# Clearing the weights above the diagonal on GpSimd in attention's last steps

## The chip, the cores and the metric

The kernel runs on one core of a Trainium2 chip. A core has TensorE for matrix products (PE in the profile, its weight loads PEld), VectorE (DVE), ScalarE (ACT), GpSimd (POOL) and SyncE (SP), which here issues most of the DMAs. TensorE writes its products to PSUM; the other tiles lie in SBUF. Each engine works through its own queue in order, and waits for the others through semaphores. The metric is the device time of one execution in microseconds; the time of a kernel is the median of its runs.

## The reference

Two layers act on x of shape (2, 1024, 512), each adding an "attention" branch and a feed-forward branch of the normalized x. Only the second layer's attention matters here. It has 16 heads of 32 numbers, and position i may look at positions j up to i:

```python
scores = jnp.einsum('bqhe,bkhe->bhqk', q, k) * scale
causal = jnp.tril(jnp.ones((l, l), dtype=bool))
scores = jnp.where(causal[None, None], scores, -jnp.inf)
attn = jax.nn.softmax(scores, axis=-1)
out = jnp.einsum('bhqk,bkhe->bqhe', attn, v)
out = out.reshape(b, l, d) @ W_out.T + b_out
```

The rest of the layer is a gated feed-forward network of width 2048, whose hidden values are thinned to two of four before the last product. The first layer has a small recurrence in place of attention, and a feed-forward network with a Walsh-Hadamard transform.

## The kernel before

The kernel has three stages, one after the other: the first layer, then attention of the second, then its feed-forward network. Attention lies between about 653 and 1211 us of the profile.

**Units and steps.** Attention works on eight units `u`, each one batch element and four heads (tiles have 128 partitions: 4 heads of 32). Scores are held transposed, keys on the partitions and queries along the row. A step `(u, j, kt)` takes one block of 128 keys, `kt`, against a half `j` of 512 queries: 4 steps for j = 0 and 8 for j = 1, so `per` = 12 a unit and 96 in all. In the last four steps of a half, `kt >= 4 * j`, the block of keys meets the diagonal: `s` is the first query that sees it, and the 128 columns from `s` on hold the triangle.

**What a step does.** `weights` (from L1218) computes the scores of four heads on TensorE into two PSUM tiles of two heads each (L1226), and subtracts the row's shift by a small product (L1232); ScalarE takes the exponential of each tile into SBUF (L1243), as `acc` in a half's first step, else as `pt`, of which there are five buffers. On the diagonal the part of the tile that lies above it is then set to 0, in one of two ways. GpSimd's `affine_select` (L1252) keeps an element where column minus row is not negative, and writes 0 elsewhere. VectorE (L1248) takes the minimum with `allowed`, a constant triangle of 1e30 and 0. One step later `gather` multiplies the weights with the values on TensorE (`o`, L1276) and adds them to the running sums `acc` (`add_weights`, L1263). At the end of a half `total` (L1296) sums over the partitions by a product with ones, ScalarE copies that to `inv` (L1301, one buffer), VectorE takes its reciprocal in four quarters (L1306), and after the fourth GpSimd multiplies the half's output `att` with it (L1308).

**Which engine.** `idle_vector(u, j, kt)` is true when the step lies within the last `ahead` = 13: by then the maxima, a pass over the scores that runs 13 steps ahead and keeps VectorE occupied, are over. Where it is true, VectorE adds the running sums, else GpSimd (with one exception). With `kt - 1` in the call, VectorE clears the triangle in steps 84 to 95, which is unit 7.

**The order.** The loop over `n` writes out every engine's order by hand: `weights` of step n, then what is put in the middle of it, `gather` of step n - 1, the maxima of step n + 13, one part of a projection (`one_part`: a part is four products, and every second part ends with VectorE's addition of the result to x, L1318), then `what_is_fixed`, which issues the reciprocals (`divide`). `in_program_order` makes every engine keep that order. For unit 7's first half `total` comes in step 89, the reciprocals in steps 89 (two), 90 and 91, and the multiplication L1308 behind the fourth, in step 91.

`allowed` is made at the start of attention by a GpSimd memset and an `affine_select` (L974, L975), between those of `mask` and the constants after it.

Of the kernel before, what the change touches and what calls it, by code (L numbers as in the profile page):

```python
# [9 lines left out]
F32 = mybir.dt.float32  # L10
BF16 = mybir.dt.bfloat16
AF = mybir.ActivationFunctionType
ALU = mybir.AluOpType
PSUM = bass.MemoryType.PSUM

P = 128
# [15 lines left out]
MASKED = -1e30  # L32
# [3 lines left out]
def two_layers(ctx: ExitStack, tc: tile.TileContext, t: dict, out: bass.AP):  # L36
    nc = tc.nc
# [32 lines left out]
    def ps_wide(name):  # L70
        nonlocal wides
        wides += 1
        return ps_pair(name, wides % 3)
# [282 lines left out]
    with tc.tile_pool(name="a", bufs=1) as a:  # L356
# [39 lines left out]
        for name in ("dskip", "Wo_by"):  # L396
            factors[name] = row(f"{name}_tmp")
            nc.sync.dma_start(
                out=factors[name],
                in_=t[name].partition_broadcast(P) if name == "dskip" else t[name],  # L400
# [387 lines left out]
        for n in range(NU - 1):  # L788
            u = 2 * n + 2
# [41 lines left out]
        for base in (0, NU):  # L831
            i, d = 2 * base // NU, base + (1 if base else 3)
# [119 lines left out]
    with tc.tile_pool(name="b", bufs=1, reuse_waits="tile") as b:  # L952
# [7 lines left out]
            out=wv, in_=t["WqkvT"][:, 2 * D :].rearrange("(k p) c -> p k c", p=P)  # L960
# [8 lines left out]
            out=mask, in_=mask, compare_op=ALU.is_ge, fill=MASKED,  # L969
            base=0, pattern=[[-1, P]], channel_multiplier=1,  # L970
        )

        allowed = b.tile([P, P], F32, name="allowed")
        nc.gpsimd.memset(allowed, -MASKED)  # L974
        nc.gpsimd.affine_select(  # L975
            out=allowed, in_=allowed, compare_op=ALU.is_ge, fill=0.0,
            base=0, pattern=[[1, P]], channel_multiplier=-1,
        )
        identb = b.tile([P, P], BF16, name="identb")
        nc.vector.tensor_copy(identb, ident)  # L980
        onesb = b.tile([P, P], BF16, name="onesb")
# [231 lines left out]
        def idle_vector(u, j, kt):  # L1213

            return per * u + 4 * j + kt + ahead >= len(second)

        def weights(u, j, kt):

            q, k, neg = qk[u, 0], qk[u, 1], negs[u, j]
            name = f"{u}_{j}_{kt}"  # L1220
            s = max(0, kt - 4 * j) * P
            cols = slice(j * 512 + s, (j + 1) * 512)
            pair = [ps_wide(f"s_{name}_{p}") for p in range(2)]
            for h in range(4):
                rows = slice(h * HD, (h + 1) * HD)
                nc.tensor.matmul(  # L1226
                    pair[h // 2][:, h % 2, s:], k[rows, kt * P : (kt + 1) * P], q[rows, cols],
                    start=True, stop=False,
                )
            for h in range(4):  # L1230
                rows = slice(h * HD, h * HD + 3)
                nc.tensor.matmul(  # L1232
                    pair[h // 2][:, h % 2, s:], onesb[rows, :], neg[rows, s:],
                    start=False, stop=True,
                )
            got = []
            for p in range(2):

                if kt == 0:
                    pt = b.tile([P, 2, 512], F32, tag=f"acc{p}", name=f"acc_{name}_{p}", bufs=2)  # L1240
                else:
                    pt = b.tile([P, 2, 512], F32, tag="pt", name=f"pt_{name}_{p}", bufs=5)
                nc.scalar.activation(  # L1243
                    pt[:, :, s:], pair[p][:, :, s:], AF.Exp, scale=1.0 / math.sqrt(HD)
                )
                d = pt[:, :, s : s + P]
                if kt >= 4 * j and idle_vector(u, j, kt - 1):
                    nc.vector.tensor_tensor(  # L1248
                        d, d, allowed.unsqueeze(1).to_broadcast([P, 2, P]), ALU.min
                    )  # L1250
                elif kt >= 4 * j:
                    nc.gpsimd.affine_select(  # L1252
                        out=d, in_=d, compare_op=ALU.is_ge, fill=0.0,
                        base=0, pattern=[[0, 2], [1, P]], channel_multiplier=-1,
                    )
                got.append(pt)
            return u, j, kt, s, got
# [208 lines left out]
        for n in range(-ahead, len(second)):  # L1466
            if n == 0:
                alone = None
            now = weights(*second[n]) if n >= 0 else None
            for f, *args in middle.pop(n, ()):  # L1470
                f(*args)
            if behind is not None:
                gather(*behind)
            behind = now
            for f, *args in after.pop(n, ()):
                f(*args)
            if n < 0:
                one_part(n)
            if n + ahead < len(first):
                do_first(n + ahead)  # L1480
            while add_later:
                add_weights(*add_later.pop())
            if (n >= 0 or n % 2) and n not in quiet:
                one_part(n)
            while late(n) and one_part(n):
                pass
            what_is_fixed(n)
# [17 lines left out]
    with tc.tile_pool(name="c", bufs=1, reuse_waits="tile") as c_:  # L1505
# [131 lines left out]
        for n in range(groups - 1):  # L1637

            end = n == groups - 2
            u = 2 * n + 2  # L1640
# [165 lines left out]
```

## Time and profile before

| | us |
|---|---|
| median of three runs (lowest, highest) | 1796.81 (1796.33, 1798.09) |
| the profiled execution | 1798.73 |
| its span, first to last instruction | 1797.0 |

Instructions of the span that have to do with the triangle and with the sums around it (us from the span's start):

| line, engine | what | count | mean or median ns | where |
|---|---|---|---|---|
| L1252 POOL | selection, 128x256 | 112 | 409 | 727 to 1151 |
| L1248 DVE | minimum, 128x256 | 16 | 422 | 1151 to 1185 |
| L1263 POOL | running sums | 124 | 1770 | 737 to 1150 |
| L1263 DVE | running sums | 36 | 949 | 784 to 1187 |
| L1306 DVE | reciprocal of a quarter, 128x128 | 8 from 1150 to 1190 | 926 | |
| L1308 POOL | multiplication by the inverse, 128x512 | 2 from 1150 to 1190 | 1272 | 1164, 1174 |

Busy time of the engines in stretches of 10 us, and the clock granted to TensorE as a share of full speed:

| us | PE | DVE | ACT | POOL | clock |
|---|---|---|---|---|---|
| 1150 to 1160 | 9.13 | 8.69 | 7.58 | 1.68 | 1.00 |
| 1160 to 1170 | 9.59 | 7.93 | 7.53 | 1.27 | 1.00 |
| 1170 to 1180 | 8.21 | 10.00 | 3.69 | 1.27 | 0.83 |
| 1180 to 1190 | 9.75 | 7.17 | 2.33 | 0.00 | 1.00 |

How to read it: times of a group are those of its instructions' records, from start to end; a record contains time that the instruction stands still after it has started. In the timeline and the chain of waits a row has a start, a duration, an engine, the operation's line and what it writes and reads; in brackets stands how long the engine was idle before it, and what ended that. In the windows `0.82 (x4)` is a busy time and a number of instructions.

### The profile page before, as it was taken

The numbers are of one execution on the slowest core, as the hardware profiler recorded it, in microseconds if no ns is written. First come the engines' busy times: TensorE is split into PE (matmuls) and PEld (weight loads), VectorE is DVE, ScalarE is ACT, GpSimd is POOL, SyncE is SP. The second block draws the span as 40 slices with busy tenths as digits, with TensorE's granted clock in tenths as the row PEclk, the third lists the DMA queues.
The fourth block names the chain that finished last, engine by engine and source line by source line (L and its number), as shares of the span: only waits on it lengthen the run. The fifth ranks groups of instructions, "written<-read, shape, count | busy, mean of one in ns | idle before, by whom it ended". The sixth has DMA issues, their size and how long they took to land.

```text
span 1797.0 us, 19003 instructions
## 1 busy us (share of the span) xinstructions
PE 1772.6 (99%) x7354; PEld 909.9 (51%) x7354; DVE 1153.1 (64%) x1516; ACT 480.3 (27%) x687; POOL 836.0 (47%) x727
## 2 busy tenths in 40 slices
PE   9999999999999999999999999999999999999999
PEld 5456566555555564333333333334555555555555
DVE  4875444555544458576666767752867778768676
ACT  3322222122221113433443443412212211212220
POOL 5145553355642244577867866613243344243510
PEclk9999999999999999999999999999999999999999
DMA  6120110111101010000000000011011102201101
GB/s 235 47 82 24 47 43 28 36 36 36 36 24 36 12 41 13 1 12 13 1 24 25 13 12 1 25 47 43 28 59 35 48 24 72 87 29 47 47 1 47
DMA packets 29609, 68.12 MB, mean 38 GB/s; under 512 B 3408, under 2 KB 11856, under 8 KB 27984
## 3 DMA queue, kind: packets, MB, share of 16 engines
q1 hardware_dynamic: 28800, 66.61, 11.1%
q8 instruction: 59, 0.97, 0.2%
q10 hardware_dynamic: 720, 0.30, 0.1%
q14 instruction: 30, 0.25, 0.0%
HBM read 62.70 MB, written 4.19 MB: 37 GB/s over the span
## 4 chain that ended last, share of the span: by engine, by line
PE 90%; POOL 4%; DVE 3%; issue 2%; ACT 1%; ACTq 0%; POOLq 0%; DVEq 0%
PE p_a L183 22%; PE p_c L183 21%; PE d L309 19%; PE m L1169 4%; PE s L1226 3%; PE pv L1047 3%; POOL acc L1263 3%; PE pq_a L1122 3%; PE po L1047 3%; PE o L1276 3%; PE dr L1627 2%; PE pq_c L1122 1%; DVE tops L1177 1%; POOL pt L1252 1%; PE pp L607 1%
## 5 line engine op out<-in xcount | busy, mean ns | idle before, releaser
L327 POOL TENSOR_TENSOR x<-x,de 128x512 f32<-128x512 f32 x87 | 126.6, 1470 | 297.8 <-DVE x L322 162.2
L1263 POOL TENSOR_TENSOR acc<-acc,pt 128x1024 f32<-128x1024 f32 (+3 forms) x124 | 216.4, 1770 | 0.0
L1177 DVE TENSOR_REDUCE tops<-m 128x2 f32<-128x1024 f32 (+2 forms) x192 | 180.9, 956 | 52.3 <-PE m L1169 47.7
L322 DVE TENSOR_TENSOR x<-x,d 128x512 f32<-128x512 f32 x145 | 99.1, 684 | 143.0 <-PE d L309 142.7
L1243 ACT ACTIVATE pt<-s 128x1024 f32<-128x1024 f32 (+3 forms) x160 | 115.3, 766 | 190.1 <-PE s L1232 171.1
L309 PE MATMUL d<-td,h 128*128 128x256 f32 x592 | 139.2, 379 | 0.0
L309 PEld LDWEIGHTS d<-td,h 128*128 128x128 f32 x592 | 112.5, 190 | 42.6 <-issue 28.7
L183 PE MATMUL p_a<-xt,s_a 128*128 128x512 f32 x256 | 116.6, 598 | 0.0
L183 PE MATMUL p_a<-xt,w 128*128 128x512 f32 x256 | 115.4, 593 | 0.7 <-ACT xt L136 0.7
L183 PE MATMUL p_c<-xt,gu 128*128 128x512 f32 x256 | 115.7, 592 | 0.0
L183 PE MATMUL p_a<-t_a,s_a 128*128 128x512 f32 x256 | 115.3, 594 | 0.0
L183 PE MATMUL p_c<-xt,s_c 128*128 128x512 f32 x256 | 115.1, 592 | 0.0
L1169 PE MATMUL m<-qk,qk 32*128 32x512 f32 (+3 forms) x768 | 102.0, 538 | 3.7 <-ACT acc L1243 3.0
L1176 DVE TENSOR_TENSOR m<-m,mask 128x256 f32<-128x256 f32 x128 | 54.8, 428 | 72.4 <-PE m L1169 63.9
L1226 PE MATMUL s<-qk,qk 32*128 32x512 f32 (+3 forms) x768 | 97.7, 532 | 3.5 <-DVE tops L1177 2.3
L176 POOL TENSOR_TENSOR s_c<-gu,s_c 128x512 f32<-128x512 f32 x16 | 20.4, 1275 | 132.4 <-PE p_c L183 132.4
L183 PEld LDWEIGHTS p_a<-xt,s_a 128*128 128x128 f32 x256 | 47.3, 190 | 57.6 <-issue 57.1
L1169 PEld LDWEIGHTS m<-qk,qk 32*128 32x128 f32 x768 | 39.6, 184 | 71.7 <-issue 25.3
L1276 PE MATMUL o<-pt,v 128*32 128x512 f32 (+3 forms) x640 | 71.1, 482 | 4.2 <-POOL pt L1252 2.1
L183 PEld LDWEIGHTS p_c<-xt,s_c 128*128 128x128 f32 x256 | 48.6, 190 | 51.4 <-issue 50.2
L183 PEld LDWEIGHTS p_c<-xt,gu 128*128 128x128 f32 x256 | 48.6, 190 | 51.0 <-issue 49.5
L183 PEld LDWEIGHTS p_a<-xt,w 128*128 128x128 f32 x256 | 48.4, 190 | 50.1 <-issue 47.6
(286 smaller groups left out, 3216.2 us busy)
## 6 DMA issues: line engine op xcount, KB each, us to landing
w<-in_W SPq DMA_DIRECT2D x32, 512.0 KB, 3.5
gu<-in_gu SPq DMA_DIRECT2D x32, 512.0 KB, 3.5
wd<-in_down SPq DMA_DIRECT2D x8, 1024.0 KB, 4.9
x<-in_x SPq DMA_DIRECT2D x16, 256.0 KB, 4.2
w2h<-in_W2q SPq DMA_DIRECT2D x4, 1024.0 KB, 11.5
xr<-in_x SPq DMA_DIRECT2D x16, 256.0 KB, 2.7
wqk<-in_WqkvT SPq DMA_DIRECT2D x16, 256.0 KB, 3.0
out_x<-x SPq DMA_DIRECT2D x15, 256.0 KB, 2.0
```

The source lines that it names most:

```text
L183: nc.tensor.matmul(pair[:, m, :], a[:, m, k, :], x[:, k, :], start=start and k == 0, stop=stop and k == 1, skip_group_check=True,)
L309: nc.tensor.matmul(out_[:, j, :], lhs[:, q, j * P : (j + 1) * P], rhs[:, q], start=m in (0, 1, 3, 4) and j == q == 0, stop=j == q == 1, sk ...
L322: nc.vector.tensor_add(r, r, out_)
L327: nc.gpsimd.tensor_add(r, r, u2[half])
L1047: nc.tensor.matmul(got[0], lhs(k), rhs(k), start=(k == 0), stop=(k == KC - 1))
L1122: nc.tensor.matmul(got[chain], lhs[:, k, :], rhs[k] if type(rhs) is list else rhs[:, k, :], start=start and k == 0, stop=stop and k == 1, ...
L1169: nc.tensor.matmul(pair[h // 2][:, h % 2, :e], q[rows, qt * P : (qt + 1) * P], k[rows, c * 512 : c * 512 + e], start=True, stop=True,)
L1177: nc.vector.tensor_reduce(out=tops[u][:, c, qt, 2 * p : 2 * p + 2], in_=pair[p][:, :, :e], axis=mybir.AxisListType.X, op=ALU.max,)
L1226: nc.tensor.matmul(pair[h // 2][:, h % 2, s:], k[rows, kt * P : (kt + 1) * P], q[rows, cols], start=True, stop=False,)
L1243: nc.scalar.activation(pt[:, :, s:], pair[p][:, :, s:], AF.Exp, scale=1.0 / math.sqrt(HD))
L1263: eng.tensor_add(acc[:, :, s:], acc[:, :, s:], pt[:, :, s:])
L1276: nc.tensor.matmul(po[rows, s:], v[:, rows], pts[h // 2][:, h % 2, s:], start=(kt == 0), stop=last, tile_position=(0, h * HD),)
```

## The change

The selections of GpSimd take the place of VectorE's minima in steps 84 to 95 too. The constant `allowed` and the two instructions that make it are gone. Nothing else is edited; running sums stay where they were.

```diff
-        allowed = b.tile([P, P], F32, name="allowed")
-        nc.gpsimd.memset(allowed, -MASKED)
-        nc.gpsimd.affine_select(
-            out=allowed, in_=allowed, compare_op=ALU.is_ge, fill=0.0,
-            base=0, pattern=[[1, P]], channel_multiplier=-1,
-        )
...
                 d = pt[:, :, s : s + P]
-                if kt >= 4 * j and idle_vector(u, j, kt - 1):
-                    nc.vector.tensor_tensor(
-                        d, d, allowed.unsqueeze(1).to_broadcast([P, 2, P]), ALU.min
-                    )
-                elif kt >= 4 * j:
+                if kt >= 4 * j:
                     nc.gpsimd.affine_select(
                         out=d, in_=d, compare_op=ALU.is_ge, fill=0.0,
                         base=0, pattern=[[0, 2], [1, P]], channel_multiplier=-1,
                     )
```

## The prediction

> **What bounds the kernel now.** I read the shares on the page first, then the chain of waits over the stretch that the change touches, then the timeline and short windows there.
>
> ```profile
> PE 1772.6 (99%) x7354; PEld 909.9 (51%) x7354; DVE 1153.1 (64%) x1516; ACT 480.3 (27%) x687; POOL 836.0 (47%) x727
> ```
>
> TensorE is busy almost throughout, so a change on VectorE and GpSimd counts only where it opens or closes a hole in TensorE's row. The edited branch runs where `per*u + 4*j + kt - 1 + 13 >= 96`, that is for steps 84 to 95, unit 7 alone. Eight of its twelve steps lie on the diagonal, with two tiles each:
>
> ```profile
> L1248 DVE TENSOR_TENSOR pt<-pt,allowed x14: 357/422/1497, 1153.6 to 1185.0; 128x256 f32<-128x256 f32 x14
> L1248 DVE TENSOR_TENSOR acc<-acc,allowed x2: 411/418/424, 1151.4 to 1151.9; 128x256 f32<-128x256 f32 x2
> L1252 POOL TENSOR_SCALAR_AFFINE_SELECT pt<-pt x98: 398/409/881, 731.7 to 1150.3; 128x256 f32<-128x256 f32 x98
> ```
>
> So 16 minima of 0.42 us go and 16 selections of 0.41 us come, on the same 128x256 elements; these lines also give the stretch, 1151 to 1186 us. The chain of waits there (start, us, what):
>
> ```profile
> 1164.02 1.28 POOL att L1308
> 1165.33 0.59 ACT inv L1301
> 1165.95 1.76 DVE inv L1306 x2
> 1167.71 1.14 DVE acc L1263 x2
> ...
> 1172.99 0.86 DVE inv L1306
> 1173.85 1.71 DVE pt L1248 x2
> 1175.60 1.92 PE o L1276 x4
> 1177.52 2.57 PE po L1047 x4
> ```
>
> The reader is to see that from 1164 to 1175.6 the end is set by VectorE (reciprocals, running sums, then the minima of step 92, two in 1.71 us), and from 1175.60 by TensorE again. GpSimd meanwhile holds little: after 1152.4 the timeline has only two multiplications by the inverse (L1308), at 1164.02 and 1173.99, until 1194. On those counts the move looks like a relief. Two things speak against it.
>
> **First: the two engines exclude each other.** The trace of before shows this where VectorE's last borrowed sum met GpSimd (start, us, engine, line):
>
> ```profile
> 1147.73 1.82 POOL L1263 TENSOR_TENSOR acc<-acc,pt 128x768 f32<-128x768 f32 x1
> 1147.82 2.28 DVE L1263 TENSOR_TENSOR acc<-acc,pt 128x512 f32<-128x512 f32 x1
> 1149.49 0.88 POOL L1252 TENSOR_SCALAR_AFFINE_SELECT pt<-pt 128x256 f32<-128x256 f32 x1
> 1150.02 0.89 DVE L1263 TENSOR_TENSOR acc<-acc,pt 128x512 f32<-128x512 f32 x1
> 1150.32 0.85 POOL L1252 TENSOR_SCALAR_AFFINE_SELECT pt<-pt 128x256 f32<-128x256 f32 x1
> ```
>
> A 128x512 sum alone takes 0.65 us (two in 1.29 us at 1158.64). Here it took 2.28: it stood still until GpSimd's sum ended at 1149.5, then ran its 0.6. The selection behind it took 0.88 instead of 0.41, and so on in turns. The Trainium skill (SBUF — State Buffer, § Who interferes with whom) states the rule: a VectorE operation with two SBUF inputs and a GpSimd operation that reads SBUF need the same port, which the first to start holds for its whole instruction; the other stands still. Read by the durations alone (0.41 us on an idle engine), the VectorE queue between 1154.9 and 1163.9 loses its four minima of steps 86 and 87. Without them: copy of the shifts 0.40, sums of step 85 2 x 0.91, of step 86 2 x 0.65, two reciprocals 1.76, sums of step 87 2 x 0.39, two reciprocals 1.76: 7.82 us, from the end of the transposes at 1154.93 to 1162.75, against 1163.88 in the trace: a gain of 1.13 us. By the rule, the four selections run between these very sums and hold them up by 0.13 + 3 x 0.40 = 1.3 us: 1164.05, a loss of 0.2. The trace's own rows above decide for the second: I take **0** here, between -1.13 and +0.2. (The first selection, from 1155.07, has mostly run when the copy ends at 1155.33, hence 0.13.) Steps 84 and 85 cost nothing: their sums have no reader until 1156, and TensorE reads the tile of step 84 at 1152.59, 1153.1 for its second half, when the selection is done at 1152.57. Selection 86's second half comes at about 1156.8 instead of 1155.98; TensorE slips by some 0.5 us there, which the wait for ACT's copy of the inverse at 1165.33 (0.36 us of TensorE idle, 1.27 of weight loads) takes up.
>
> **Second: the queue of GpSimd.** The multiplication of unit 7's first half is issued in step 91, after the reciprocal of its last quarter, and the selections of step 92 stand behind it in GpSimd's queue. In before:
>
> ```profile
> 1173.99 1.27 POOL L1308 TENSOR_TENSOR att<-att,inv 128x512 f32<-128x512 f32 x1 [8.70 <-ACT pt L1243]
> 1174.05 1.50 DVE L1248 TENSOR_TENSOR pt<-pt,allowed 128x256 f32<-128x256 f32 x1
> ```
>
> The first minimum slipped in ahead of it (1173.77 to 1174.13), the second waited for it and ended at 1175.55. After the change, with times of before and strict turns:
> - The last reciprocal ends at 1173.8. Next on VectorE is a sum of step 91 (1.17 us, its tile ready since 1170.03); it takes the lock at once: to 1174.95.
> - The multiplication has it next: 1.27, to 1176.2.
> - The other sum, waiting since 1174.95: to 1177.4.
> - Selection of step 92, first half: to 1177.8; second half, nothing between: to 1178.2.
>
> So TensorE's second half of o starts at 1178.2 in place of 1175.60: **+2.6 us**, the first half at 1177.8 in place of 1174.18. TensorE has nothing else: its order puts o of step 92 ahead of the projection. Behind it, in one queue, wait o, the four projection products, and the scores of step 94.
>
> **What hangs on it: the clock.** (windows of 1 us: us, busy of PE, PEld, DVE, ACT, POOL, then the granted clock)
>
> ```profile
> 1173.00:1174.00 1.00, 0.00 (x0) 0.00 (x0) 1.00 (x2) 0.81 (x1) 0.01 (x1) 1.00 0.00 0
> 1174.00:1175.00 1.00, 0.82 (x4) 0.14 (x4) 1.00 (x2) 0.00 (x0) 1.00 (x1) 1.00 0.00 0
> 1175.00:1176.00 1.00, 0.64 (x4) 0.19 (x4) 1.00 (x2) 0.00 (x0) 0.27 (x1) 0.69 0.00 0
> 1176.00:1177.00 1.00, 1.00 (x4) 0.00 (x0) 1.00 (x2) 0.20 (x1) 0.00 (x0) 0.50 0.00 0
> ```
>
> The granted clock is 0.50 from about 1175.4 to 1178.8, and o's last four matmuls take 1.92 us where all eight take 1.06 at 1170.45, the four projection products 2.64 where others take 1.98: some 2 us are lost to the clock in before already. Afterwards TensorE is idle from 1172.75 to 1177.8, 5.1 us, so it resumes at half clock too. The Trainium skill (TensorE: Matmul & The Clock Gate, Part 1) has a free-running window of 3.4 us, after which the rate is set by how busy it was; the 3.4 us of this trace agree. If the window in which it resumes counts as idle, a second half-rate window follows. Half of 3.4 us, 1.7, is the most that this adds; the least is 0 (or a little below, if the two losses differ by phase). I take 0.4, near the low end, because before carries such a loss already and both depend on the phase.
>
> **Given back.** At 1184.85 a projection waited 0.25 us for VectorE's addition at L1318; with TensorE late, it has waited out: -0.25. The remaining sums (steps 92 to 95) run in turns with selections: 0.4 us each, but the sums end at about 1189.1 and the product of ones with them (L1296) stands at 1189.03 + 2.7 in TensorE's order, so they stay hidden; were they 2.6 us later still, they would be paid one for one. The tail has no other hole: TensorE runs without a gap from 1190 to 1221, and GpSimd's weight sums, done at 1200.66, are needed at 1214.
>
> **The removed constant** is a 0.21 us memset and a 0.30 us selection on GpSimd at 653, before an idle time of 2.19 us on that engine: 0. Its 512 bytes per partition shift the tiles allocated after it; no row bears on what this does, and I count nothing.
>
> **Sum:** 0 + 2.6 + 0.4 - 0.25 = +2.7 us (bounds: -0.6 with no lock; +4.4 with the whole clock window and 0.2 in the first part). The profiled execution took 1798.73 us (span 1797.0 and 1.73 around it), so 1801.4 by itself; it is the slow end of the runs shown, whose median is 1796.81. Against the median: **1799.5 us**.
>
> **The rivals.**
> - *Second cold window* (24%): as above with the full 1.7 us of clock: +4.0 to +4.4, 1801.1. For it: the window from 1175.4 to 1178.8 would hold 1 us of TensorE work of 3.4, and the one before it, with 1.6, was followed by half rate. Against: its phase is free.
> - *The multiplication goes first* (16%): GpSimd keeps the lock from its multiplication (1173.99 to 1175.26) through both selections, to 1176.05: +0.45 us at o, 1797.2. Against: the turns at 1149 to 1151.
> - *Relief, not slower* (10%): if selections and sums do run side by side, the last reciprocal comes 1.13 us earlier, the multiplication ends at 1174.1, the selections at 1174.5 and 1174.95, o's second half 0.6 us earlier; and if the shorter hole saves half the clock loss, -1.5: 1795.3. It decides as soon as selections beside sums last 0.41 us and not 0.8. For it: 6.7 us of work leave a full engine. Against: the 2.28 us row.
> - *As worked out* (50%): +1.5 to +3.5.
>
> **Numbers.** 0.2% is 3.6 us, about what a measurement can tell from no change: slower than 1800.4, faster than 1793.2. The second cold window and the top of the forecast's spread are beyond it on the slow side: 0.30. Faster needs more than all of TensorE's idle time from 1150 to 1190 (40 us less a busy time of 9.13 + 9.59 + 8.21 + 9.75 by 10 us windows: 3.3 us): 0.03. The rest, 0.67, is within. The range from 1795.9 to 1801.6 leaves out the most favourable half of the relief and the worst clock phases.
>
> **What would show it.** L1252 gains 16 instances from 1151 to 1190, many at 0.7 us or more; sums on VectorE beside them above 1.17 us; reciprocals of 1164 and 1173.8 within 0.3 us of where they were; the multiplication at 1174 at over 2 us, o of step 92 waiting on GpSimd until about 1178; a longer stretch at half clock. I am wrong if the multiplication at 1174 takes 1.27 us, if o starts before 1176, if the reciprocals come a microsecond early, or if the difference arises outside 1150 to 1195.

## The result: slower by 0.14%, and the profile after

| | before | after |
|---|---|---|
| median, 20 runs each, us | 1798.45 | 1801.63 |
| lowest to highest, us | 1796.29 to 1802.14 | 1798.85 to 1804.27 |
| span of the profiled execution, us | 1797.0 | 1799.4 |

The ratio is 1.0014, with a 95% interval from 1.0008 to 1.0021: 2.5 us more, which is also the difference of the means (the medians lie 3.2 us apart). Forecast were 2.7, from a median of 1796.81 that was taken over three runs; over twenty, the kernel before lies 1.6 us higher. So the absolute 1799.5 is 2.1 us low, mostly for that, and the measured median, 1801.63, stands at the upper end of the range up to 1801.6 that was laid around 1796.81.

Where the time went is measured from a point that the change can't touch, the start of step 83's first selection on GpSimd, to one where TensorE alone sets the pace again, the first gate-up product. I call this the stretch: 1149.49 to 1210.73, **61.24 us** before; 1149.79 to 1213.13, **63.34 us** after. Of the 2.4 us between the spans, 2.1 arise in it, 0.3 before it. The chain of waits of the kernel after (start, us, what; lines below the edit have moved up by 7 or 11, so L1252 is the running sum, L1295 the reciprocal, L1265 `o`):

```profile
1172.33 0.14 DVE inv L1295
1172.47 0.72 issue
1173.19 1.17 DVE acc L1252
...
1175.43 1.40 POOL pt L1241
1176.83 0.04 issue
1176.87 2.28 PE o L1265 x8
1179.15 3.26 PE po L1040 x4
```

Behind the last reciprocal there stood a minimum before; now a sum follows, then GpSimd's selections, and `o` of step 92 starts at 1176.87. Why so late, the timeline of both engines shows (start, us, engine, line):

```profile
1173.19 1.16 DVE L1252 TENSOR_TENSOR acc<-acc,pt 128x1024 f32<-128x1024 f32 x1
1173.42 2.05 POOL L1297 TENSOR_TENSOR att<-att,inv 128x512 f32<-128x512 f32 x1 [8.70 <-ACT pt L1236]
1174.27 2.28 DVE L1252 TENSOR_TENSOR acc<-acc,pt 128x1024 f32<-128x1024 f32 x1
1175.43 1.39 POOL L1241 TENSOR_SCALAR_AFFINE_SELECT pt<-pt 128x256 f32<-128x256 f32 x1
```

The sum takes the lock first, the multiplication stands still for it (2.05 us in place of 1.27), the second sum for the multiplication (2.28 in place of 1.17), the first selection for that sum (1.39 in place of 0.41). ScalarE had finished both tiles of step 92 at 1172.40, a microsecond before the multiplication started and while GpSimd stood idle; but GpSimd works in order, so the selections came behind all of it. TensorE over this time (windows: us, busy of PE, PEld, DVE, ACT, POOL, granted clock):

```profile
1173.00:1174.00 1.00, 0.00 (x0) 0.00 (x0) 1.00 (x2) 0.32 (x1) 0.58 (x1) 1.00 0.00 0
1174.00:1175.00 1.00, 0.00 (x0) 0.00 (x0) 1.00 (x2) 0.55 (x1) 1.00 (x1) 1.00 0.00 0
1175.00:1176.00 1.00, 0.00 (x0) 0.00 (x0) 1.00 (x1) 0.26 (x1) 1.00 (x2) 0.50 0.00 0
1176.00:1177.00 1.00, 0.13 (x2) 0.13 (x4) 0.70 (x2) 0.00 (x0) 1.00 (x2) 0.50 0.00 0
...
1181.00:1182.00 1.00, 1.00 (x3) 0.29 (x1) 0.54 (x1) 0.00 (x0) 0.00 (x0) 0.59 0.00 0
1182.00:1183.00 1.00, 1.00 (x13) 0.42 (x12) 0.00 (x0) 0.00 (x0) 0.00 (x0) 1.00 0.00 0
```

Idle for 4.45 us, it resumes at half clock and stays there until about 1181.8: twice as long as before.

### The profile page after: what moved, and what is told of

It is laid out like the page before. It is cut to its first block, busy times and chain, and to the rows that moved or that the text cites. A ratio compares the mean times of both kernels' runs of the same rounds, so it can differ in the third digit from the quotient of the medians.

```text
span 1799.4 us, 19017 instructions
## 1 busy us (share of the span) xinstructions
PE 1774.4 (99%) x7354; PEld 911.5 (51%) x7354; DVE 1150.1 (64%) x1500; ACT 480.3 (27%) x687; POOL 847.3 (47%) x741
## 4 chain that ended last, share of the span: by engine, by line
PE 91%; POOL 4%; DVE 2%; issue 2%; ACT 1%; POOLq 0%; ACTq 0%; DVEq 0%
PE p_a L183 22%; PE p_c L183 21%; PE d L309 19%; PE m L1162 4%; PE s L1219 4%; PE pv L1040 3%; PE pq_a L1115 3%; PE o L1265 3%; PE po L1040 2%; PE dr L1616 2%; POOL acc L1252 2%; PE pq_c L1115 1%; DVE tops L1170 1%; PE pp L607 1%; PE pw L443 1%
## 5 line engine op out<-in xcount | busy, mean ns | idle before, releaser
L1252 POOL TENSOR_TENSOR acc<-acc,pt 128x1024 f32<-128x1024 f32 (+3 forms) x124 | 216.2, 1768 | 0.0
L1265 PE MATMUL o<-pt,v 128*32 128x512 f32 (+3 forms) x640 | 70.6, 482 | 6.3 <-POOL pt L1241 6.1
L1241 POOL TENSOR_SCALAR_AFFINE_SELECT pt<-pt 128x256 f32<-128x256 f32 x112 | 52.0, 480 | 49.4 <-ACT pt L1236 48.5
```

The source lines that it names most:

```text
L1252: eng.tensor_add(acc[:, :, s:], acc[:, :, s:], pt[:, :, s:])
L1265: nc.tensor.matmul(po[rows, s:], v[:, rows], pts[h // 2][:, h % 2, s:], start=(kt == 0), stop=last, tile_position=(0, h * HD),)
```

## The experiments

Theory: the loss is the queue of GpSimd, that is step 92's selections behind the multiplication, with the clock after the hole. Rival A: the lock by itself, at every selection that runs beside a sum. Rival B: the constant that is gone, with all addresses behind it. Each run gives the stretch from its profile, and a ratio to runs of the kernel before.

| kernel | stretch, us | clock in the stretch | median, us | ratio, 95% interval |
|---|---|---|---|---|
| before | 61.24 | half for 3.4 us | 1798.45 | |
| before_again | 61.77 | half for 3.4 us | 1800.59 | 1.0006 [0.9999, 1.0014] |
| before_kept_busy | 60.18 | full | 1799.04 | 1.0002 [0.9994, 1.0010] |
| before_mult_later | 60.19 | full | 1797.92 | 0.9999 [0.9991, 1.0007] |
| after | 63.34 | half for 6.8 us | 1801.63 | 1.0014 [1.0008, 1.0021] |
| constant_kept | 62.74 | half for 3.4 us | 1803.00 | 1.0018 [1.0012, 1.0025] |
| kept_busy | 64.19 | full | 1803.51 | 1.0026 [1.0016, 1.0035] |
| kept_busy_5 | 61.17 | full | 1800.38 | 1.0001 [0.9992, 1.0009] |
| first_half | 59.34 | full | 1798.79 | 0.9995 [0.9987, 1.0004] |
| second_half | 64.14 | half for 6.8 us | 1802.43 | 1.0023 [1.0014, 1.0031] |
| mult_later | 58.77 | full | 1796.65 | 0.9995 [0.9987, 1.0004] |
| mult_later_2 | 58.79 | full | 1796.87 | 0.9987 [0.9981, 0.9994] |
| mult_on_vector | 57.92 | full | 1796.31 | 0.9987 [0.9980, 0.9993] |

The runs of before that these ratios rest on have medians from 1798.09 to 1799.15. Where a stretch has no half clock, stretches can be compared directly; the kernel before then takes 60.2 us (before_kept_busy, before_mult_later).

**One half at a time.** In the kernel before, VectorE's branch was narrowed to one half of the queries, so that GpSimd selects in the other, the one in the label:

```diff
-                if kt >= 4 * j and idle_vector(u, j, kt - 1):
+                if kt >= 4 * j and j and idle_vector(u, j, kt - 1):        # first_half
+                if kt >= 4 * j and not j and idle_vector(u, j, kt - 1):    # second_half
```

> Selections on GpSimd in steps 84 to 87 only, minima on VectorE in steps 92 to 95, the constant kept. The stretch is measured in the profile from the start of step 83's first selection to the first gate-up product: 61.24 us before, 63.34 us after. Theory (queue of GpSimd: the loss is the selections of step 92 standing behind the multiplication by the inverse, and TensorE's clock after the hole): VectorE is relieved in the first half, the last reciprocal some 0.9 us earlier, o of step 92 second half by as much; stretch about 60.3 us, time 0 to 1 us under before. Rival A (the lock alone: every selection beside a sum costs): half of the loss, stretch about 62.3. Rival B (the removed constant and the addresses behind it): as before, 61.2.

> Selections on GpSimd in steps 92 to 95 only, minima on VectorE in steps 84 to 87, the constant kept. Theory (queue): the whole loss without the 0.9 us relief of the first half, stretch about 64.2 us, time about 3 us over before; the multiplication at the end of step 91 lasts about 2 us and o of step 92 waits for GpSimd. Rival A (lock alone): half of the loss, stretch about 62.3. Rival B (constant): 61.2.

The first half is no loss: 59.34, which against the kernel before at full clock (60.19) is a relief of 0.85 us, as expected; its ratio can't be told from 1, but compared at the same granted clock (see *The clock*) its runs lie 0.9 us under before. The second half is the whole loss and more, 64.14. (That profile, like before_again, has another order at step 83: VectorE waits there through two sums and two selections of GpSimd, and the stretch is 0.5 us longer; against before_again the second half costs 2.4.) Rival A wanted a loss in both halves. In the first half GpSimd's queue holds nothing that waits for VectorE's last work: selections run beside sums there too, and the last reciprocal still ends earlier.

**The constant.** In the kernel after, made as before and not used:

```diff
+        allowed = b.tile([P, P], F32, name="allowed")
+        nc.gpsimd.memset(allowed, -MASKED)
+        nc.gpsimd.affine_select(out=allowed, in_=allowed, ...)
```

> The kernel after, with the unused constant still made, so that all addresses and GpSimd's work at the start of attention are as before. Theory (queue) and rival A (lock): as after, stretch 63.3 us within 0.5, time about 2.5 us over before. Rival B (constant): as before, stretch 61.2.

62.74 and 1.0018: as after, but for a clock that came back after 3.4 us in its profile. Rival B falls; both constants and addresses are the same as before here, and the loss is there.

**The queue.** The multiplication of unit 7's first half was put behind step 92's selections, in the kernel after and in the one before, and then given to VectorE:

```diff
-            if q == 3:
-                nc.gpsimd.tensor_mul(att[u, j], att[u, j], inv[u, j])
+            if q == 3 and (u, j) != (len(units) - 1, 0):
+                multiply(u, j)
...
+                    if (u, j) == (len(units) - 1, 0):
+                        put(n + 3, multiply, u, j)
```

```diff
-                nc.gpsimd.tensor_mul(att[u, j], att[u, j], inv[u, j])
+                eng = nc.vector if (u, j) == (len(units) - 1, 0) else nc.gpsimd
+                eng.tensor_mul(att[u, j], att[u, j], inv[u, j])
```

> The kernel after, with unit 7's first multiplication by the inverse issued at the end of step 92, behind that step's selections. Theory (queue): the selections of step 92 run as soon as their exponentials are there, o of step 92 starts some 3 to 4 us earlier than after, the hole of TensorE closes to about 1 us and the clock stays at 1.00; stretch 58 to 60 us, time 1 to 3 us under before. Rival A (lock alone): the selections still run beside sums, stretch about 63. Rival B (constant): 63.3.

> The kernel before (minima on VectorE), with unit 7's first multiplication issued at the end of step 92. Theory: the second minimum of step 92 no longer stands still for it (0.4 us in place of 1.5), o of step 92 starts 1.1 us earlier, stretch 59 to 60.2 us (the less if the clock stays full); the order of the queue matters in both kernels, and with it put right the selections on GpSimd are the faster by some 0.5 to 1.5 us (58.8 there). Rival (VectorE is the better engine for this in any order): below 58.8.

> The kernel after, with unit 7's first multiplication by the inverse on VectorE, behind its reciprocals; GpSimd's queue has nothing ahead of the selections of steps 92 and 93. Theory (queue): as mult_later, o of step 92 starts at about 23 us behind step 83's first selection, stretch 58 to 59 us, time 1 to 2.5 us under before. Rival (the lock alone): selections still run beside sums: stretch 62 to 63, time as after.

> mult_later once more, unchanged, to narrow its interval: ratio 0.9985 to 0.9995, so that both series together lie under 1 (theory); rival: 1.000 or more.

Both orders close the hole. In the timeline of mult_on_vector:

```profile
1173.51 1.63 POOL L1241 TENSOR_SCALAR_AFFINE_SELECT pt<-pt 128x256 f32<-128x256 f32 x2 [6.69 <-ACT pt L1236]
1174.43 0.94 DVE L1295 RECIPROCAL inv<-inv 128x128 f32<-128x128 f32 x1
1174.83 1.41 PE L1265 MATMUL o<-pt,v 128*32 128x512 f32 x8 [0.33 <-POOL pt L1241]
1175.41 0.69 DVE L1298 TENSOR_TENSOR att<-att,inv 128x512 f32<-128x512 f32 x1
```

The selections start before the last reciprocal and end beside it, not behind what depends on it; `o` starts 22.96 us behind the stretch's start (27.08 in after), having waited 0.33 us (4.45 in after). mult_on_vector also takes the multiplication off GpSimd; mult_later does not, and changes the place alone:

```profile
1172.02 1.62 POOL L1241 TENSOR_SCALAR_AFFINE_SELECT pt<-pt 128x256 f32<-128x256 f32 x2 [6.69 <-ACT pt L1236]
1173.96 2.12 POOL L1300 TENSOR_TENSOR att<-att,inv 128x512 f32<-128x512 f32 x1 [0.32 <-ACT pt L1236]
```

`o` starts at 22.96 us there too, though the multiplication still stands still for a sum (2.12 us) and so do later selections (1.38 to 1.40, as in after). So rival A can't have it. With 57.92 us and a ratio of 0.9987 [0.9980, 0.9993] mult_on_vector beats both kernels, and mult_later does too in its second series; in the first its interval held 1.

My expectation of before_mult_later was wrong. The later place in the program changed nothing: 60.19 us, as before_kept_busy (60.18), and `o` starts where it does in before (24.67 and 24.69 us behind the stretch's start). In its timeline the pair of minima still takes what it took:

```profile
1178.43 1.78 DVE L1248 TENSOR_TENSOR pt<-pt,allowed 128x256 f32<-128x256 f32 x2
```

GpSimd has nothing else to do in that kernel, so the multiplication starts as soon as the reciprocal is done, wherever it stands in the order, and holds the second minimum up. An order in a queue matters only to what is queued with it.

**The clock.** Products that nobody reads, put on TensorE just ahead of `o` of step 92 (nine in kept_busy, five in kept_busy_5, three in before_kept_busy):

```diff
+            if n == len(second) - 3:
+                spare = ps_bank("spare", 1)
+                for _ in range(5):
+                    nc.tensor.matmul(spare, ident, wout[:, 0, :], start=True, stop=True)
             if behind is not None:
                 gather(*behind)
```

> The kernel after, with nine products of 128x512 without a reader put on TensorE between the scores of step 93 and o of step 92, where it stands idle for 4.4 us. Theory (the hole costs time of its own and by the clock): o and the projection behind it run at full clock, 3.1 us together in place of 5.5; stretch (first selection of step 83 to first gate-up product) about 60.9 us in place of 63.3; time some 2 us under the kernel after. Rival (the clock is no cause, TensorE is late only by the wait): 63.3.

> The kernel before with three such products in the same place. Theory: before loses about 2 us to the clock too, when a window falls badly; stretch about 59.3 us in place of 61.2, and 1.2 to 1.5 under kept_busy, which is the loss of the change with the clock taken out. Rival (clock no cause): 61.2.

> As kept_busy, with five products: nine filled 8 us, since each is two instructions of 0.44 us, and held o back themselves. Five fill 4.4 us, as long as the hole. Theory: o of step 92 starts where it does after (27.1 us behind step 83's first selection), at full clock; stretch about 61 us in place of 63.3, against 60.2 of the kernel before at full clock; mean granted clock over the runs as before (0.9983) instead of after (0.9970); time 0.5 to 1.5 us over before. Rival (the clock is no cause of the loss): 63.3, and time as after.

kept_busy was a mistake of size: nine products filled 8 us and kept `o` itself waiting, hence 64.19. With five (timeline of kept_busy_5, whose stretch starts at 1149.59):

```profile
1172.16 4.56 PE L1464 MATMUL spare<-wout,ident 128*128 128x512 f32 x10
1176.71 1.41 PE L1265 MATMUL o<-pt,v 128*32 128x512 f32 x8
1178.05 1.98 PE L1040 MATMUL po<-wout,att 128*128 128x512 f32 x4
```

`o` starts 27.12 us behind the stretch's start, as in the kernel after (27.08), but takes 1.41 us in place of 2.28, and the projection 1.98 in place of 3.33: 61.17 us. So of the 3.15 us by which the stretch of after exceeds that of before at full clock (60.19), **1.0 are the wait and 2.2 the clock**. The kernel before had 1.05 of clock loss in its own profile; before_kept_busy, at 60.18, took away that much and not the 2 us expected. The ratio of kept_busy_5 can't be told from 1.

One profile is one phase of the clock; the runs give an average. Each run has its granted clock, and 140 runs of before in the three series are sorted by it. Their means are 1796.57 us at 1.000 (26 runs), 1797.90 at 0.999 (36), 1799.34 at 0.998 (34), 1800.94 at 0.997 (31), 1801.97 at 0.996 (12), and one run at 0.995; about 1.35 us for each 0.001. The profiles show what 0.001 is: half clock comes in them for 3.41 us or twice that, and 3.41 us at half take 0.00095 off the mean. It comes at other places too (in before at 977, in before_kept_busy at 24, 857 and 980), so a run's clock counts all of these, about two in a run of before and three in one of after. In before, with the columns as above:

```profile
978.00:979.00 1.00, 1.00 (x8) 0.52 (x8) 0.00 (x0) 0.47 (x2) 0.93 (x3) 0.50 0.00 0
```

The mean granted clock is 0.9982 before, 0.9970 after and 0.9985 in kept_busy_5. The difference of 0.0012 makes 1.6 us. The wait makes the rest: compared with before at the same granted clock, the 20 runs of after lie 0.8 us higher and those of kept_busy_5 1.1. Together 2.4 to 2.7, against the measured 2.5. The part of the clock is the less certain: before_again, the kernel before unchanged, had a mean of 0.9975 in its 13 runs, so such a mean can be off by 0.0007, or 0.9 us. But all three kernels with the long hole have the lowest clocks of all (after 0.9970, second_half 0.9967, constant_kept 0.9964). The same comparison at equal clock puts mult_later 1.3 and 1.2 us under before, mult_on_vector 1.7 under, and before_mult_later and before_again within 0.1 of it.

**The kernel before, again.**

> The kernel before, unchanged, for a second profile at another phase of the clock. Theory: same starts on VectorE and GpSimd within 0.1 us of the stretch's start, stretch 59.2 (no loss to the clock) to 61.4 us; ratio 1.000. Rival (the 2.1 us between the two stretches was chance): 63 or more.

61.77 us, a little above the 61.4 expected, with the clock at half for 3.4 us and the other order at step 83: two profiles of one kernel differ by half a microsecond here. The loss of after is no chance of one profile, but thirteen runs of an unchanged kernel can have a median (1800.59) 2.5 us above that of its series (1798.09), as much as the change costs; the ratio's interval holds 1. At step 83 (start, us, engine, line):

```profile
1145.95 3.58 POOL L1263 TENSOR_TENSOR acc<-acc,pt 128x768 f32<-128x768 f32 x2
1146.60 3.68 DVE L1187 TENSOR_TENSOR tops<-tops 128x16 f32<-128x16 f32 x1
1149.48 0.78 POOL L1252 TENSOR_SCALAR_AFFINE_SELECT pt<-pt 128x256 f32<-128x256 f32 x2
```

VectorE's small operation, which in before waits for the first sum alone (1.22 us), stands still until GpSimd's two sums and two selections are over at 1150.26. So the two engines need not take turns: here the one that waited was passed over three times.

## Why the prediction was right, by its steps

- **The place, the queue, and what would show it**: shown, but for one sign. The multiplication was to take over 2 us (2.05), sums beside it to be held up (2.28), `o` to wait for GpSimd, the half clock to last longer, and nothing to arise outside the stretch (0.3 us did). The order of turns (sum, multiplication, sum, selection) came as written. mult_later takes away only the place in the queue, and the loss goes with it. The sign that failed: the last reciprocal was to stay within 0.3 us of its place and came 0.87 earlier.
- **"The two engines exclude each other", first half, taken as 0**: a relief of 0.87 us (multiplication at 1163.45 less 0.30, against 1164.02). Both of its sizes were off, in the same direction. VectorE before, with the minima of step 87 between the sums, and after:

```profile
1156.23 1.82 DVE L1263 TENSOR_TENSOR acc<-acc,pt 128x768 f32<-128x768 f32 x2
1157.97 0.75 DVE L1248 TENSOR_TENSOR pt<-pt,allowed 128x256 f32<-128x256 f32 x2
1158.64 1.29 DVE L1263 TENSOR_TENSOR acc<-acc,pt 128x512 f32<-128x512 f32 x2
1159.84 0.94 DVE L1306 RECIPROCAL inv<-inv 128x128 f32<-128x128 f32 x1
```

```profile
1155.53 3.82 DVE L1252 TENSOR_TENSOR acc<-acc,pt 128x768 f32<-128x768 f32 x4
1159.27 0.94 DVE L1295 RECIPROCAL inv<-inv 128x128 f32<-128x128 f32 x1
```

Four selections were to hold the sums up by 1.3 us. From the first start to the operation behind them, the four sums took 1.74 + 1.20 us before and 3.74 after: 0.80. A selection stands still for much of a sum (0.85 to 1.08 us in place of 0.41), but a 128x768 sum beside it took 1.13 in place of 0.95. And the queue without minima was summed from durations, 7.82 us; consecutive records overlap, and from start to start its operations take 7.3, so that the minima were worth some 1.7 us and not 1.13.

- **"+2.6 us" at `o`**: mis-sized. Less the 0.30 us by which the stretch starts later, step 92's selections were done at 1176.88, not at 1178.2: +1.28 against 1175.60. Of the 1.3 us between, 0.8 are the earlier chain, the rest are shorter steps behind it: the multiplication ended 1.12 us after the sum that held it up, not 1.27, and the selection 0.27 us after its sum, not 0.41. With what VectorE's addition gave back (-0.25 was taken), kept_busy_5 shows 1.0 us net.
- **"I take 0.4" for the clock**: 1.6 us on the average of the runs, 1.1 between the two profiles. The loss that before already had was taken for some 2 us and is 1.05. The rival with a second cold window had this right, at up to 1.7: in after, the window in which TensorE resumed held 1.5 us of its records in 3.4, and a second half-rate window followed; in constant_kept the half-rate window began 0.34 us after `o` had started, was full of work, and no second followed. That rival got 24%, and its clock belonged into the forecast. The window ahead of before's half rate held 1.8 us, not the 1.6 that was read for it.
- **Sum**: 0 + 2.6 - 0.25 for the waits against 1.0, and 0.4 for the clock against 1.6. The errors had opposite signs; that 2.7 came so near to 2.5 is luck. (The upper bound adds up to 4.25, not 4.4.)
- *Relief* was real in the first half, but smaller than the queue's loss. *The multiplication goes first* did not happen: here the turns held. **The removed constant** at 0: shown by constant_kept.

## What to carry to other kernels

Before moving work to an engine that looks idle, write down what stands ahead of it in that engine's queue and what that waits for: here one multiplication, which waits for the busy engine that was to be relieved, made a full engine's relief into a loss, and moving it behind made it a gain. The hole of 4.45 us in TensorE was paid twice, once as the wait and once in the clock, and the clock's part depends on a phase that differed from profile to profile: compare runs at the same granted clock before a microsecond is believed. Where two engines exclude each other, count the holds from the trace and from start to start, as less than a whole instruction may be lost.

## What was not expected of the hardware

- The spread of the kernel's times, 1796 to 1803 us, is nearly all clock: sorted by granted clock, the 140 runs of before fall on one line of 1.35 us for 0.001, that is for about one stay of 3.41 us at half rate.
- The hold is not the same on both sides. VectorE's sums were held up by some 0.2 us for each selection of 0.41, half of what a lock for the whole instruction would cost, and by 1.1 us for the multiplication of 1.27; GpSimd's selections by 0.4 to 1.0 us. Who comes next is no strict turn either (step 83 in before_again and second_half).
- TensorE takes an f32 product of 128x512 as two instructions that start 0.44 us apart (ten for five in kept_busy_5), which is why nine of them filled 8 us. The four instructions of a projection part, called four products above, are two products in the kernel.
